# Working out the nodes' order in six pieces across a tile loop, with VectorE's order in that loop kept as written

## The chip, the cores and the metric

One NeuronCore of a Trainium2 chip runs the whole program. The metric is the device time in microseconds of one execution; lower is better. A profile of one further execution, with its own time, goes with it.

## What is computed

Four graph layers over 2048 nodes, 8 batches and 64 features, each with a residual and a layer normalization. The change concerns the first layer only, in which each node belongs to some of 64 hyperedges (`H` is 2048 x 64, zeros and ones):

```python
h = x @ W
s = leaky_relu(h @ a_node, 0.2)
alpha = softmax(where(H.T[None] > 0, s[:, None, :], NEG), axis=-1)
agg = einsum('ben,bnf->bef', alpha, h)
beta = sigmoid((h @ a_gn)[:, None, :] + (agg @ a_ge)[:, :, None])
all_he = elu(beta[..., None] * h[:, None] + (1 - beta[..., None]) * agg[:, :, None])
...
g = einsum('bne,benf->bnf', softmax(where(H[None] > 0, se[:, None, :], NEG), axis=-1), all_he)
```

The later layers multiply by the 2048 x 2048 adjacency matrix many times; they are most of the kernel's time.

## The kernel before

The 2048 nodes are 16 tiles of 128. The loop over h (lines 597 to 644, called the loop from here) takes one tile t in each turn:

- Four fp32 matmuls on TensorE (line 601) make `ph`, the products h of all eight batches with the two score columns beside them. `ph` has two buffers in PSUM, so tile t+2 can start only when tile t's `ph` has been read.
- VectorE clips the scores into `seen` (611), makes the leaky scores `lr` (618), writes (h+1) times an exponential into the staging tile `st` (624), and h times another exponential into `ex` (628). ScalarE (ACT) makes the two exponentials: `e_gn` out of `seen` (616), which `st` needs, and the column of `ex` out of `lr` (622), which `ex` needs.
- GpSimd (POOL) casts the tile's slot numbers into `st` (614).
- After every second tile, ACT's queue writes `st` to `hs_hbm` in memory (634). `st` has three buffers of two tiles each.
- Four matmuls (636) add the tile's part to `pagg`, the sums over the nodes of each hyperedge.
- At tiles 1, 3, 5, 7 and 9 POOL copies one element of `seen` (482) and then issues a load of part of the adjacency matrix (211): loads are paced by the loop in this way. At tiles 9 and 11 `parts` casts a piece of x on ACT (`v0h`, `v1h`, line 167) and subtracts on POOL (`v0l`, `v1l`, line 168).

A later stage handles nodes in the order of how many hyperedges they belong to, since nodes with few need few steps. `rank` (line 532) is each node's position in that order. `place()` (lines 553 to 590) turns it around: it finds for each node the tile `tl` of its position and the place `q` within it, makes the one-hot `ohq` (128 x 16 x 128) of the places, and the values `val` (the node's tile number and row, each under its `tl`). Sixteen small matmuls (582) sum `val` over the nodes into `po`, and `order` (589) holds, for each position, the node that belongs there. Everything but those matmuls is on VectorE. `place()` is called once, at tile 9 (line 631). `order` is read by the gathers of rows of `hs_hbm` (line 275), which POOL issues after the loop, and by the scatters of that later stage.

The program is written in a framework that decides itself in which sequence an engine gets its instructions, by their dependences and its own estimates. `tc.keep_in_program_order` marks an instruction to be kept in the sequence of the program among the others that are so marked. Before the change, in the loop, these are ACT's second exponential (622), POOL's paced copies and loads, the casts and subtractions of `parts(0, c)`, and the first instruction of `place()` (558); VectorE's four operations of a tile are not marked.

Of the kernel before, what the change touches and what calls it, by code (L numbers as in the profile page):

```python
# [30 lines left out]
F32 = mybir.dt.float32  # L31
F32R = mybir.dt.float32r
BF16 = mybir.dt.bfloat16
# [4 lines left out]
ALU = mybir.AluOpType  # L38
AX = mybir.AxisListType
# [17 lines left out]
def tile_gnn_fast(  # L57
# [24 lines left out]
    nc = tc.nc  # L82
# [3 lines left out]
    P = 128  # L86
    NT = N // P
# [116 lines left out]
    order = hy.tile([P, NT], U32, name="order")  # L204
# [4 lines left out]
    def load_adj(t, g):  # L209

        tc.keep_in_program_order(nc.gpsimd.dma_start(adj[t][g], adj_t[t * P:(t + 1) * P, cols(g, N // 2)]))
# [119 lines left out]
    xc, part = {}, {}  # L331
# [7 lines left out]
    def parts(p, c):  # L339
        part[c] = split(va, xc.pop((p, c)), f"v{c}", 1, [P, JT, P], nc.gpsimd, p == 0)  # L340
# [94 lines left out]
    with tc.tile_pool(name="pa_ps", bufs=1, space=PSUM) as pps:  # L435
# [17 lines left out]
        def fetch_xt(t):  # L453

            if t < NT:
                if t % (2 * XB) < XB:
                    xt[t] = xs.tile([P, NP, P], F32, tag="xt", name="xt", bufs=XB)
                else:
                    xt[t] = va.tile([P, NP, P], F32, tag=("v2h", "v2l", "v3h", "v3l")[t % XB], name="xt", bufs=1)
                nc.sync.dma_start(xt[t], x_t[t])  # L460
# [3 lines left out]
        so_scope = ExitStack()  # L464
        so = so_scope.enter_context(tc.tile_pool(name="so", bufs=1))
# [4 lines left out]
        iota = so.tile([P, P], BF16, name="iota")  # L470
        nc.gpsimd.iota(iota, [[1, P]], base=0, channel_multiplier=0, allow_small_or_imprecise_dtypes=True)
        row = so.tile([P, 1], F32, name="row")
# [8 lines left out]
        def behind(what):  # L481
            tc.keep_in_program_order(nc.gpsimd.tensor_copy(seen_x, what))
# [13 lines left out]
        for b in range(2):  # L496
# [21 lines left out]
            flat, lhsT=tri, rhs=oh.rearrange("p t b -> p (t b)"), start=True, stop=False  # L518
        )
        for t in range(NT - 1):  # L520
            nc.tensor.matmul(
                flat[:, (t + 1) * BINS:], lhsT=ones_b,
                rhs=oh[:, t:t + 1, :].to_broadcast([P, NT - 1 - t, BINS]), start=False, stop=False,
            )
        nc.tensor.matmul(
            flat, lhsT=ones_b, rhs=gtb[:, None, :].to_broadcast(bins), start=False, stop=True
# [4 lines left out]
        rank = so.tile([P, NT], F32, name="rank")  # L531
        nc.vector.tensor_reduce(rank, gt, AX.X, ALU.add)

        over = so.tile([P, BINS], F32, name="over")
# [9 lines left out]
        for t in range(NT // 2):  # L544
            for k in range(2):
                r = slice(k * E, (k + 1) * E)
# [6 lines left out]
        def place():  # L553

            tl = so.tile([P, NT], F32, name="tl")
            ge = so.tile([P, NT, NT], F32, name="ge")
            tc.keep_in_program_order(
                nc.vector.tensor_scalar(over[:, 0:NT], iota[:, 0:NT], float(P), -0.5, op0=ALU.mult, op1=ALU.add)
            )
            wide = [P, NT, NT]  # L560
            nc.vector.tensor_tensor(
                ge, rank[:, :, None].to_broadcast(wide), over[:, None, 0:NT].to_broadcast(wide), ALU.is_gt
            )
            nc.vector.tensor_reduce(tl, ge, AX.X, ALU.add)
            nc.vector.tensor_scalar(tl, tl, -1.0, None, op0=ALU.add)
            q = so.tile([P, NT], F32, name="q")
            nc.vector.scalar_tensor_tensor(q, tl, -float(P), rank, op0=ALU.mult, op1=ALU.add)
            nc.vector.tensor_tensor(
                ge, tl[:, :, None].to_broadcast(wide), iota[:, None, 0:NT].to_broadcast(wide), ALU.is_equal
            )  # L570
            val = so.tile([P, NT, 2, NT], BF16, name="val")
            nc.vector.tensor_tensor(
                val[:, :, 0, :], ge, iota[:, 0:NT, None].to_broadcast(wide), ALU.mult
            )
            nc.vector.tensor_scalar(val[:, :, 1, :], ge, row, None, op0=ALU.mult)
            po = pps.tile([P, 2, NT], F32, tag="sm", name="po", bufs=2)
            ohq = so.tile([P, NT, P], BF16, name="ohq")
            nc.vector.tensor_tensor(
                ohq, q[:, :, None].to_broadcast([P, NT, P]), iota[:, None, :].to_broadcast([P, NT, P]), ALU.is_equal
            )  # L580
            for t in range(NT):
                nc.tensor.matmul(
                    po.rearrange("p i t -> p (i t)"), lhsT=ohq[:, t, :],
                    rhs=val[:, t].rearrange("p i t -> p (i t)"), start=t == 0, stop=t == NT - 1,
                )
            olo = so.tile([P, NT], F32, name="olo")
            nc.vector.tensor_copy(olo, po[:, 1, :])

            nc.vector.scalar_tensor_tensor(order, olo, float(NT), po[:, 0, :], op0=ALU.mult, op1=ALU.add)
            so_scope.close()  # L590


        seen = pa.tile([P, NT, B, 2], F32, name="seen")

        pagg = pps.tile([P, C], F32, tag="agg", name="pagg", bufs=1)
        G = B // 2
        for t in range(NT):
            ph = pph.tile([P, 2, C], F32, tag="ph", name="ph", bufs=2)
            ph8 = ph.rearrange("p k (g c) -> p (k g) c", c=P)
            for p in range(NP):  # L600
                nc.tensor.matmul(
                    ph8[:, 2 * p:2 * p + 2, 0:F + 2], lhsT=xt[t][:, p, :], rhs=bd66, start=True, stop=True
                )
            fetch_xt(t + 2 * XB)
            hv = ph8.rearrange("p (k g) c -> p k g c", k=2)
            if t % 2 == 0:
                st2 = pa.tile([P, 2, HROW], F32, tag="st", name="st", bufs=3)
            st = st2[:, t % 2]
            ex = pa.tile([P, 2, G, F + 1], F32, tag="ex", name="ex", bufs=2)
            sv = seen[:, t].rearrange("p (k g) c -> p k g c", k=2)  # L610
            nc.vector.tensor_scalar(
                sv, hv[:, :, :, F:F + 2], CLIP, -CLIP, op0=ALU.min, op1=ALU.max
            )
            nc.gpsimd.tensor_copy(st[:, BF + 8:], slot[:, t, :])
            e_gn = st[:, BF:BF + 8]
            nc.scalar.activation(e_gn.rearrange("p (k g) -> p k g", k=2), sv[:, :, :, 1], AF.Exp)
            lr = pa.tile([P, B], F32, tag="lr", name="lr", bufs=2)
            nc.vector.scalar_tensor_tensor(
                lr, seen[:, t, :, 0], 0.2, seen[:, t, :, 0], op0=ALU.mult, op1=ALU.max
            )  # L620
            tc.keep_in_program_order(
                nc.scalar.activation(ex[:, :, :, F], lr.rearrange("p (k g) -> p k g", k=2), AF.Exp)
            )
            nc.vector.scalar_tensor_tensor(
                st[:, 0:BF].rearrange("p (g f) -> p g f", f=F), ph8[:, :, 0:F], 1.0,
                e_gn[:, :, None].to_broadcast([P, B, F]), op0=ALU.add, op1=ALU.mult,
            )
            nc.vector.tensor_tensor(
                ex[:, :, :, 0:F], hv[:, :, :, 0:F], ex[:, :, :, F:F + 1].to_broadcast([P, 2, G, F]), ALU.mult
            )  # L630
            if t == 9:
                place()
            if t % 2:
                nc.scalar.dma_start(hs_hbm.rearrange("(p t) c -> p t c", t=NT)[:, t - 1:t + 1, :], st2)
            for k in range(2):
                nc.tensor.matmul(
                    pagg[k * E:(k + 1) * E, 0:G * (F + 1)], lhsT=m_n[:, t, :], rhs=ex[:, k].rearrange("p g c -> p (g c)"),
                    start=t == 0, stop=t == NT - 1,
                )
            if t in paced:  # L640
                behind(seen[:, t, 0, 0:1])
                load_adj(paced[t], 0)
            if t in (9, 11):
                parts(0, (t - 9) // 2)
# [25 lines left out]

        gv = pagg[:, 0:G * (F + 1)].rearrange("p (g c) -> p g c", c=F + 1)
        den = ta.tile([P, G], F32, name="den")
        nc.vector.tensor_scalar(den, gv[:, :, F], 1.0e-30, None, op0=ALU.max)
        nc.vector.reciprocal(den, den)
        agg = ta.tile([P, G, F], F32, name="agg")
        nc.vector.tensor_tensor(agg, gv[:, :, 0:F], den[:, :, None].to_broadcast([P, G, F]), ALU.mult)
# [64 lines left out]
    with ExitStack() as pb_scope:  # L741
        pps = pb_scope.enter_context(tc.tile_pool(name="pb_ps", bufs=1, space=PSUM))
# [94 lines left out]
    pin = tc.keep_in_program_order  # L837
# [505 lines left out]
    def load_raw(k, place):  # L1343
        raw[k] = xnp.tile(wide_w, F32, tag=f"xn{place}", name="raw")
        pin(nc.sync.dma_start(raw[k], w_8[k]))
# [415 lines left out]
    place = ["g"] * NCH  # L1761
# [63 lines left out]
    for p in range(NP):  # L1825
# [3 lines left out]
        for step in range(STEPS):  # L1829
# [4 lines left out]
            for g in range(2):  # L1834
# [16 lines left out]
                for mine in ([[c] for c in own] if very_end else [own]):  # L1851
                    for t in range(NT if p or step else 0):
                        if checks and t in (2, 7, 12):
                            check()
                        for i in range(2):
                            for c in mine:
                                mm(
                                    u[c], lhsT=x_part[t // JT][i][:, t % JT, :], rhs=adj_c(t, c),
                                    start=False, stop=t == NT - 1 and i == 1,
# [765 lines left out]
```

## Time and profile before

| what | value |
|---|---|
| time, median of 3 runs | 1736.24 us (1735.61, 1736.24, 1749.89) |
| profiled execution: its own time | 1743.63 us |
| profiled execution: span | 1741.8 us |
| mean granted clock of TensorE | 0.987 |
| first `seen` of the loop | at 14.77 us |
| last `ex` of the loop ends | at 56.26 us |
| place(): first instruction to end of `order` | 34.40 to 42.04 us |
| first gather of rows (POOL) | issued at 59.39 us |
| DMA, 16.4 to 36.5 us | 382 GB/s, share 1.06 |

Times in the profile are counted from the start of the span. PE is TensorE's matmuls, PEld its weight loads, DVE is VectorE, ACT ScalarE, POOL GpSimd; SPq, ACTq and POOLq are the queues in which DMAs are issued. L624 is line 624 of the kernel. An entry such as `st<-ph,st 128x512` names the tile written, the tiles read, and the partitions and elements. The idle time in brackets lies before the instruction on its engine, with what ended it. A duration can overlap the start of the next instruction on the same engine a little. The granted clock is the share of TensorE's full clock that it was given.

### The profile page before, as it was taken

The numbers are of one execution on the slowest core, as the hardware profiler recorded it, in microseconds if no ns is written. First come the engines' busy times: TensorE is split into PE (matmuls) and PEld (weight loads), VectorE is DVE, ScalarE is ACT, GpSimd is POOL, SyncE is SP. The second block draws the span as 40 slices with busy tenths as digits, with TensorE's granted clock in tenths as the row PEclk, the third lists the DMA queues.
The fourth block names the chain that finished last, engine by engine and source line by source line (L and its number), as shares of the span: only waits on it lengthen the run. The fifth ranks groups of instructions, "written<-read, shape, count | busy, mean of one in ns | idle before, by whom it ended". The sixth has DMA issues, their size and how long they took to land. (4 is left out here: it accounts for less than half of the span.)

```text
span 1741.8 us, 27973 instructions
## 1 busy us (share of the span) xinstructions
PE 1659.0 (95%) x11196; PEld 1208.1 (69%) x11196; DVE 833.1 (48%) x1531; ACT 589.4 (34%) x1031; POOL 572.4 (33%) x515
## 2 busy tenths in 40 slices
PE   6889899999989999999999999999989999999996
PEld 4657666666664444468788878888767877878775
DVE  7678945677742221210127247777623433433332
ACT  1345533434322211112123267878512222212221
POOL 4578845566534444422023001322310200202001
PEclk9899999999999999999999999999999999999998
DMA  9744334444340000017344367575671121211211
GB/s 336 252 158 124 107 123 145 139 147 132 107 151 6 30 7 24 25 54 291 120 143 124 109 152 159 131 171 123 157 265 43 51 59 43 61 48 42 57 43 39
DMA packets 171180, 195.83 MB, mean 112 GB/s; under 512 B 71536, under 2 KB 116336, under 8 KB 169760
## 3 DMA queue, kind: packets, MB, share of 16 engines
q1 hardware_dynamic: 160096, 154.54, 30.5%
q0 software_dynamic: 8544, 30.68, 5.3%
q10 hardware_dynamic: 2400, 8.72, 1.3%
q8 instruction: 90, 1.47, 0.4%
q14 instruction: 50, 0.41, 0.1%
HBM read 126.72 MB, written 67.17 MB: 111 GB/s over the span
## 5 line engine op out<-in xcount | busy, mean ns | idle before, releaser
L172 PE MATMUL ua<-pt,xn 128*128 128x512 f32 x512 | 230.2, 592 | 1.4 <-DVE pt L1151 1.4
L172 PEld LDWEIGHTS ua<-pt,xn 128*128 128x128 f32 x512 | 96.9, 190 | 111.1 <-issue 104.0
L1516 DVE COPY w_half<-pw 128x512 f32<-128x512 f32 x160 | 109.7, 705 | 86.2 <-PE pw L172 85.4
L1512 ACT COPY w_half<-pw 128x1024 f32<-128x1024 f32 x128 | 129.9, 1015 | 56.9 <-PE pw L172 56.8
L172 PE MATMUL py<-w_half,xg 128*32 128x128 f32 x4096 | 142.2, 279 | 1.2 <-issue 1.2
L172 PE MATMUL u<-adj,v0h 128*128 128x512 f32 x384 | 134.5, 428 | 1.1 <-ACT h L1820 1.1
L172 PE MATMUL u<-adj_more,v2h 128*128 128x512 f32 x384 | 126.1, 406 | 0.0
L172 PE MATMUL u<-adj,v0l 128*128 128x512 f32 x384 | 125.0, 403 | 0.0
L172 PEld LDWEIGHTS py<-w_half,xg 128*32 128x32 f32 x4096 | 111.3, 138 | 18.8 <-issue 1.9
L172 PE MATMUL u<-adj_more,v2l 128*128 128x512 f32 x384 | 124.3, 401 | 0.0
L1157 POOL TENSOR_TENSOR acc<-acc,pt 128x512 f32<-128x512 f32 x60 | 76.5, 1274 | 104.3 <-DVE pt L1151 103.6
L172 PE MATMUL pw<-est,wst 64*128 64x256 f32 x1024 | 110.0, 317 | 0.7 <-ACT w_half L1512 0.4
L1151 DVE TENSOR_SCALAR pt<-pt 128x512 f32<-128x512 f32 x64 | 29.9, 466 | 152.4 <-ACT pt L1150 152.3
L172 PEld LDWEIGHTS pw<-est,wst 64*128 64x128 f32 x1024 | 82.2, 184 | 25.6 <-ACT w_half L1512 18.4
L1729 ACT CAST ar<-fcav 128x512 fp32r<-128x512 f32 x64 | 39.6, 618 | 168.9 <-DMA fcav<-in_adj_t 168.0
L1730 DVE SCALAR_TENSOR_TENSOR ar<-fcav,ar 128x512 f32<-128x512 f32 x64 | 45.8, 715 | 102.4 <-ACT ar L1729 102.4
L172 PE MATMUL u<-adj_more,v3l 128*128 128x512 f32 x288 | 93.1, 399 | 1.2 <-DVE v3l L168 1.2
L172 PE MATMUL u<-adj,v1h 128*128 128x512 f32 x288 | 93.7, 403 | 0.0
L1150 ACT ACTIVATE pt<-s 128x512 f32<-128x512 f32 x64 | 38.0, 598 | 164.5 <-PE s L172 164.5
L172 PE MATMUL u<-adj_more,v3h 128*128 128x512 f32 x288 | 92.7, 400 | 0.0
L172 PE MATMUL u<-adj,v1l 128*128 128x512 f32 x288 | 92.0, 397 | 0.0
L1701 POOL TENSOR_TENSOR x<-x,rows 128x512 f32<-128x512 f32 x16 | 22.5, 1430 | 211.4 <-PE pt L175 127.8
(408 smaller groups left out, 3275.7 us busy)
## 6 DMA issues: line engine op xcount, KB each, us to landing
fcav<-in_adj_t SPq DMA_DIRECT2D x64, 256.0 KB, 3.0
u_hbm<-ut SPq DMA_DIRECT2D x48, 256.0 KB, 3.7
xg<-u_hbm SPq DMA_DIRECT2D x24, 512.0 KB, 7.7
adj<-in_adj_t POOLq DMA_DIRECT2D x16, 512.0 KB, 7.8
adj_more<-in_adj_t POOLq DMA_DIRECT2D x16, 512.0 KB, 9.8
adj_hbm<-adj_more SPq DMA_DIRECT2D x16, 512.0 KB, 6.2
x_hbm<-r SPq DMA_DIRECT2D x28, 256.0 KB, 2.3
hs_hbm<-st ACTq DMA_DIRECT2D x8, 584.0 KB, 4.8
```

The costliest lines, as they stand in the source:

```text
L172: tc.keep_in_program_order(nc.tensor.matmul(*args, **kw))
L1150: nc.scalar.activation(pt, s, AF.Exp)
L1151: nc.vector.tensor_scalar(pt, pt, 1.0, None, op0=ALU.max)
L1157: nc.gpsimd.tensor_tensor(accs[c], accs[c], pt, ALU.add)
L1512: pin(nc.scalar.copy(dst, pw.rearrange("p j o n -> p n (j o)")))
L1516: pin(copy(dst[:, :, 2 * j:2 * j + 2], bank.rearrange("p o n -> p n o")))
L1701: nc.gpsimd.tensor_tensor(xs, xs, b2.to_broadcast([P, JT, P]), ALU.add)
L1729: nc.scalar.copy(ar, seen_a)
L1730: nc.vector.scalar_tensor_tensor(ar.bitcast(F32), seen_a, 1.0, ar.bitcast(F32), op0=ALU.mult, op1=ALU.not_equal, accum_out=left[:, t, k:k ...
```

## The change

`place()` no longer emits its instructions at once. It is called before the loop, allocates its tiles, and returns six functions under the numbers of the tiles at whose end, behind `ex`, they are called: 8 (the tile of each position), 9 (the place in it, and the first half of `val`), 10 (the second half of `val`, and `ohq` for eight tiles), 11 (`ohq` for the other eight), 12 (the sixteen matmuls), 13 (`order`). `ohq` is made by two instructions instead of one. All VectorE instructions of these pieces, and the four of each tile in the loop, are marked to be kept in program order. Cut to its core:

```diff
-            tc.keep_in_program_order(
-                nc.vector.tensor_scalar(over[:, 0:NT], iota[:, 0:NT], float(P), -0.5, op0=ALU.mult, op1=ALU.add)
-            )
...
+            def tiles_of():
+                pin(nc.vector.tensor_scalar(
+                    over[:, 0:NT], iota[:, 0:NT], float(P), -0.5, op0=ALU.mult, op1=ALU.add
+                ))
+                pin(nc.vector.tensor_tensor(
+                    ge, rank[:, :, None].to_broadcast(wide), over[:, None, 0:NT].to_broadcast(wide), ALU.is_gt
+                ))
+                pin(nc.vector.tensor_reduce(tl, ge, AX.X, ALU.add))
+
+            def places_of():
+                pin(nc.vector.tensor_scalar(tl, tl, -1.0, None, op0=ALU.add))
+                pin(nc.vector.scalar_tensor_tensor(q, tl, -float(P), rank, op0=ALU.mult, op1=ALU.add))
+                pin(nc.vector.tensor_tensor(
+                    ge, tl[:, :, None].to_broadcast(wide), iota[:, None, 0:NT].to_broadcast(wide), ALU.is_equal
+                ))
+                pin(nc.vector.tensor_tensor(
+                    val[:, :, 0, :], ge, iota[:, 0:NT, None].to_broadcast(wide), ALU.mult
+                ))
+
+            def columns(part):
+                if part == 0:
+                    pin(nc.vector.tensor_scalar(val[:, :, 1, :], ge, row, None, op0=ALU.mult))
+                n = NT // 2
+                r = slice(part * n, (part + 1) * n)
+                pin(nc.vector.tensor_tensor(
+                    ohq[:, r, :], q[:, r, None].to_broadcast([P, n, P]), iota[:, None, :].to_broadcast([P, n, P]),
+                    ALU.is_equal,
+                ))
+
+            def sum_up():
+                for t in range(NT):
+                    nc.tensor.matmul(
+                        po.rearrange("p i t -> p (i t)"), lhsT=ohq[:, t, :],
+                        rhs=val[:, t].rearrange("p i t -> p (i t)"), start=t == 0, stop=t == NT - 1,
+                    )
+
+            def order_of():
+                pin(nc.vector.tensor_copy(olo, po[:, 1, :]))
+
+                pin(nc.vector.scalar_tensor_tensor(
+                    order, olo, float(NT), po[:, 0, :], op0=ALU.mult, op1=ALU.add
+                ))
+                so_scope.close()
+
+            return {
+                8: tiles_of, 9: places_of, 10: lambda: columns(0), 11: lambda: columns(1), 12: sum_up, 13: order_of
+            }
...
+        steps_of = place()
+        pin = tc.keep_in_program_order
         for t in range(NT):
...
-            nc.vector.tensor_scalar(
+            pin(nc.vector.tensor_scalar(
                 sv, hv[:, :, :, F:F + 2], CLIP, -CLIP, op0=ALU.min, op1=ALU.max
-            )
+            ))
...
-            if t == 9:
-                place()
+            if t in steps_of:
+                steps_of[t]()
```

The other three VectorE instructions of a tile (618, 624, 628) are wrapped in `pin` in the same way.

## The prediction

> **What bounds the kernel now.** I read the page first, then the order of time around the changed code, then the granted clock in short stretches, then the list of who waited for whom.
>
> The page, its head and TensorE's row of forty slices:
>
> ```profile
> span 1741.8 us, 27973 instructions
> ...
> PE 1659.0 (95%) x11196; PEld 1208.1 (69%) x11196; DVE 833.1 (48%) x1531; ACT 589.4 (34%) x1031; POOL 572.4 (33%) x515
> ...
> PE   6889899999989999999999999999989999999996
> ```
>
> TensorE bounds the kernel nearly everywhere, but not in the first slices of 43.5 us, and the loop over h runs from 14.8 to 56.3 us. What can be won lies in those 41 us. The order of time inside the loop (start, duration, engine, line; the bracket is idle time and its releaser):
>
> ```profile
> 34.40 0.17 DVE L558 TENSOR_SCALAR over<-iota 128x16 f32<-128x16 bf16 x1
> ...
> 36.32 2.32 DVE L578 TENSOR_TENSOR ohq<-q,iota 128x2048 bf16<-128x2048 f32 x1
> 36.53 2.20 POOL L614 CAST st<-slot 128x64 f32<-128x64 bf16 x1
> 38.57 1.68 DVE L572 TENSOR_TENSOR val<-ge,iota 128x256 bf16<-128x256 f32 x1
> ...
> 38.71 1.25 POOL L168 TENSOR_TENSOR v0l<-xc,v0h 128x512 fp32r<-128x512 f32 x1
> ...
> 41.88 0.16 DVE L589 SCALAR_TENSOR_TENSOR order<-olo,po 128x16 uint32<-128x16 f32 x1
> ...
> 45.25 0.17 DVE L611 TENSOR_SCALAR seen<-ph 128x16 f32<-128x16 f32 x1 [1.56 <-PE ph L601]
> ...
> 47.65 0.17 DVE L611 TENSOR_SCALAR seen<-ph 128x16 f32<-128x16 f32 x1 [2.02 <-PE ph L601]
> ...
> 47.96 0.69 DVE L624 SCALAR_TENSOR_TENSOR st<-ph,st 128x512 f32<-128x512 f32 x1
> ```
>
> Two things are to be seen. The order of the nodes holds VectorE from 34.40 to 42.04, and tile 10's st and ex stand behind it. And VectorE's sequence is not that of the program: it takes seen of tile 12 at 45.25, then waits for tile 13's ph, and only at 47.96 does tile 12's st. The same happens at the start: seen of tile 0 is at 14.77, seen of tile 1 at 16.38, st of tile 0 only at 16.67. From tile 4 to tile 8 the sequence is the program's, and seen goes from 23.39 to 30.62: 1.81 us a tile.
>
> TensorE in stretches of about 3.4 us (busy us and count of PE, PEld, DVE, ACT, POOL; granted clock; share of DMA; GB/s):
>
> ```profile
> 36.50:39.90 3.40, 0.00 (x0) 0.10 (x1) 3.40 (x2) 0.00 (x0) 3.40 (x3) 1.00 1.01 375
> 39.90:43.30 3.40, 1.87 (x21) 0.99 (x21) 3.21 (x10) 0.43 (x2) 0.47 (x3) 0.50 0.42 130
> 43.30:46.75 3.45, 3.45 (x14) 2.44 (x15) 0.73 (x3) 1.04 (x3) 1.27 (x1) 0.50 0.53 188
> 46.75:50.16 3.41, 1.71 (x14) 1.13 (x13) 2.48 (x6) 0.42 (x2) 0.00 (x0) 1.00 0.20 65
> 50.16:53.60 3.44, 3.44 (x15) 2.44 (x15) 1.86 (x5) 0.42 (x2) 0.00 (x0) 0.51 0.45 179
> 53.60:57.00 3.40, 2.00 (x16) 1.02 (x14) 1.92 (x6) 1.31 (x4) 0.00 (x0) 1.00 0.14 56
> ```
>
> After a stretch without matmuls the clock is 0.50 for two stretches; after one with 1.71 of 3.41 us busy (50%) it is 0.51 for one; after 2.00 of 3.40 (59%) it stays at 1.00. At half clock the eight ph matmuls of two tiles take 2.13 us instead of 1.17, the four of pagg 1.14 instead of 0.66. The waits between 14 and 57 us add up what this costs:
>
> ```profile
> DVE seen L611 <- PE ph L601: 8.5, 10, 2.0
> ...
> PE pagg L636 <- DVE ex L628: 6.5, 6, 1.7
> ...
> PE po L582 <- DVE val L575: 4.2, 1, 4.2
> ```
>
> VectorE and TensorE stand waiting for each other in turn. From seen of tile 8 (30.62) to the end of ex of tile 15 (56.26) are 25.64 us, where eight tiles at 1.81 would take 14.5.
>
> [...] L572, [...] took 1.68 us while v0l ran for 1.25 on POOL, where the 256 elements of L568 took 0.42, and the cast at 36.53 took 2.20 beside ohq. [...]
>
> **The change, part by part.** No instruction goes except that ohq becomes two; no DMA is added or dropped.
>
> *Pieces.* Durations by the rows of before: tile 8 gets 0.17+0.42+0.42 = 1.01 us; tile 9 0.17+0.17+0.42+0.42 = 1.18 (0.42 for L572 without its stall, as for L568); tile 10 0.34+1.22 = 1.56; tile 11 1.22; tile 12 sixteen small matmuls, 0.59 on TensorE (half of that at full clock by ratio, about 0.3, beside VectorE's 1.63 for the tile: nothing taken; uncovered it would be 0.6); tile 13 0.17+0.16 = 0.33. Where VectorE has a piece it no longer waits for ph: a tile's four operations take 0.21+0.21+0.61+0.60 = 1.63 start to start, so 0.18 of the 1.81 is cover for a piece.
>
> *Locks.* The ACT order puts the v0h cast (0.62) behind ex of tile 9, so v0l runs beside tile 9's piece[...]: I take the full 1.25. v1l comes likewise at tile 11's half of ohq; either POOL waits (nothing) or VectorE (1.25); I take 0.6. Bounds: 0 to 2.5. The casts of slot, 0.24 each, run several tiles ahead and hide.
>
> *Periods, clock full.* Tile 8: 1.81+1.01-0.18 = 2.64; 9: 1.81+1.18-0.18+1.25 = 4.06; 10: 3.19; 11: 1.81+1.22-0.18+0.6 = 3.45; 12: 1.81; 13: 1.96; 14: 1.81; 15 to the end of ex: 1.63. Sum 20.6 us.
>
> *Clock.* TensorE's work for a tile is 0.59+1.10 = 1.69 warm: 64% of tile 8's period, 42, 53 and 49% of the next. By the 50 and 59% above, the clock falls somewhere in 9 to 11. There it costs nothing as long as VectorE takes as long as TensorE's 3.14 (1.06+2.08) at half clock; afterwards one tile runs at 3.14 instead of 1.81: 1.3 us. Bounds: 0 and, in all of tiles 12 to 14, 4.0.
>
> *Fixed order.* In the tail it is in the periods already. At the start, ex of tile 0 can end at about 16.5 instead of 17.95, so ph of tile 2 starts at 17.2 instead of 18.59: 1.4 us. But DMA is busy at a share of 1.06 with 382 GB/s from 16.4 to 36.5, and st buffers come free by the hs writes (the cast of tile 6 waited 3.4 us for one, landing just ahead of its tile at 26.92). I take half, 0.7; bounds 0 and 1.4. Kept in order, a waiting VectorE instruction holds all behind it: if st waits for a write of hs, the next seen waits, and behind it ACT's exponentials and POOL's paced loads.
>
> *Sum.* 25.64 - 20.6 - 1.3 + 0.7 = 4.4 us less. What follows the loop starts from its end: pagg of tile 15 (56.32), the normalization on VectorE, and the last write of hs (issued at 55.74), behind which POOL holds both gathers of rows (59.39) and the remaining adjacency loads (64.36). order is then ready many us before the gather. I see nothing that holds to an absolute time, so I carry 4.4 through: span 1741.8 to 1737.4, the profiled execution 1743.63 to 1739.2; the median of the runs, 1736.24, lies 7.4 below that execution, and becomes 1731.8.
>
> **Rivals.**
> *More than that.* No lock stall (1.85 less), full clock (1.3 less), all of the start (0.7 more): 8.3 us, 1728. For it: in the steady part POOL's casts cost VectorE nothing visible. Against: 42% busy at tile 9 is below what dropped the clock before.
> *Hidden anyway.* The loop is shorter but the start's gain is lost to DMA and the clock stays halved through tiles 12 to 14: 25.64-20.6-4.0 = 1.0 us, 1735.2. For it: the DMA share of 1.06. Against: from 53.6 the share is only 0.14, so the last write of hs is not crowded.
> *Slower.* The clock is at half from tile 8 on and in the first window behind the loop: TensorE's 3.14 becomes the least period. 3.14+4.06+3.19+4.1+3.74+3.14+3.14+1.63 = 26.1 us (full locks, po's 0.6 uncovered), 0.5 over today, less the start's 0.7, plus 1.7 for one halved window of 3.4 in the next stage: 1.5 over, 1737.8. It decides once every window from tile 8 to behind the loop is halved; one full window that TensorE needs brings it back to even. For it: four tiles of low TensorE load in a row. Against: today's clock recovers after one full window.
> *Not as said.* If VectorE's sequence did not follow the program, only the pieces would be spread: about the second rival.
>
> **How the numbers follow.** Forecast (2.5 to 6 us less) 0.60; more 0.12; hidden 0.15; slower 0.13. Range: from 1727 (the second bound of gain and a little run spread) to 1740 (the slower case, and part of the spread of the runs shown, 1735.61 to 1749.89). The likeliest case alone gives 1730 to 1734. One per cent, 17.4 us, is about what a measurement can tell from no change, and no case above reaches it; I leave 0.02 on each side for a rearrangement of the later instructions that aren't kept in order, which I can't price, and 0.96 between.
>
> **What would show it.** Right: no seen before the tile's own st and ex are done; the end of ex of tile 15 near 51.9; a first drop of the clock around tiles 9 to 11; L572 or L568 long beside v0l. Wrong: the loop's end moves but hrow's gather does not; st waits for a write of hs and stops VectorE; or the stage from 66 us on takes longer by what the loop won.

## The result and the profile after

The kernel after takes 1735.3 us (median of 22 runs, 1727.48 to 1741.74); the kernel before took 1740.74 on the same chip (22 runs, 1735.61 to 1749.89). The ratio is 0.9971 with a 95% interval of 0.996 to 0.9981, which is 5.05 us less (1740.74 times 0.0029), within 1%. The forecast was 4.4 us less. Its 1731.8 us for the median stands 3.5 us too low all the same, since it counts from a median of three runs, 1736.24, and 22 runs of the kernel before give 1740.74. The profiled execution after took 1736.35 us with a span of 1734.6 and a mean granted clock of 0.987.

The page of the kernel after, its head and TensorE's row of slices:

```profile
span 1734.6 us, 27974 instructions
...
PE 1656.1 (95%) x11196; PEld 1206.1 (70%) x11196; DVE 833.3 (48%) x1532; ACT 589.4 (34%) x1031; POOL 570.6 (33%) x515
...
PE   6889899999989999999999999999989999999996
```

Nothing of size can be seen here: one instruction more, the same digits in all forty slices. The change has to be looked for in the loop. The order of time there (start, duration, engine, line; L580 to L604 are the pieces, L641 is lr, L647 st, L651 ex, L275 the gather):

```profile
34.78 0.43 DVE L580 TENSOR_TENSOR val<-ge,iota 128x256 bf16<-128x256 f32 x1
...
36.83 1.87 DVE L586 TENSOR_SCALAR val<-ge,row 128x256 bf16<-128x256 f32 x1
...
37.24 1.29 POOL L168 TENSOR_TENSOR v0l<-xc,v0h 128x512 fp32r<-128x512 f32 x1
38.61 1.21 DVE L589 TENSOR_TENSOR ohq<-q,iota 128x1024 bf16<-128x1024 f32 x1
...
42.02 1.72 POOL L168 TENSOR_TENSOR v1l<-xc,v1h 128x512 fp32r<-128x512 f32 x1 [1.92 <-ACT v1h L167]
...
42.73 1.03 DVE L641 SCALAR_TENSOR_TENSOR lr<-seen 128x8 f32<-128x8 f32 x1
...
46.73 0.17 DVE L604 SCALAR_TENSOR_TENSOR order<-olo,po 128x16 uint32<-128x16 f32 x1
...
49.73 0.68 DVE L651 TENSOR_TENSOR ex<-ph,ex 128x512 f32<-128x512 f32 x1
...
53.54 1.22 POOL L275 DMA_INDIRECT hrow<-hs_hbm,order  x1 [9.80 <-DVE he L702]
```

`order` is finished 4.9 us later than before (46.90 against 42.04) and nobody minds: its first user, the gather, comes at 53.54. What counts is the last ex, which ends at 50.41 instead of 56.26, and the gather follows it by the same 3.13 us as before. Half of ohq takes 1.21; the forecast's 1.22 was its author's estimate (slot, L551, a VectorE instruction of 128x1024 too, took 1.22 in the profile of before). The two long entries on VectorE, 1.87 for L586 and 1.03 for L641, are its stalls beside POOL's v0l and v1l: L586 took 0.34 in vl_vector, where no subtraction runs beside it, and lr takes 0.17 at the next tiles.

The waits of the kernel after between 14 and 57 us (in total, times, longest), in the kernel before the three lines had 5.6, 6.5 and 8.5 us in total:

```profile
POOL st L637 <- DMA hs_hbm<-st: 12.7, 5, 4.6
...
PE pagg L659 <- DVE ex L651: 8.3, 9, 1.4
...
DVE seen L634 <- PE ph L624: 0.7, 4, 0.2
```

VectorE has nearly stopped waiting for TensorE (0.7 us after 8.5); TensorE waits for VectorE a little more (8.3 after 6.5). VectorE is the bound of the loop now: it is busy for 32.5 of its 36.5 us, TensorE for 26.7. POOL's wait for the writes of hs has doubled; at one tile it reaches VectorE (order of time, tile 6):

```profile
25.80 0.21 ACT L639 ACTIVATE st<-seen 128x8 f32<-128x8 f32 x1 [2.37 <-DMA hs_hbm<-st]
25.84 0.42 POOL L637 CAST st<-slot 128x64 f32<-128x64 bf16 x2 [4.62 <-DMA hs_hbm<-st]
...
26.10 0.69 DVE L647 SCALAR_TENSOR_TENSOR st<-ph,st 128x512 f32<-128x512 f32 x1 [1.10 <-ACT st L639]
```

ACT waits for a free buffer of st, and VectorE's st waits 1.10 us for ACT.

The granted clock (columns as in the prediction). In each of the fourteen profiles every change of the clock lies on a grid with a step of 3.41 us, and where that grid lies differs from one execution to the next (a window starts at 33.17 us in one profile of the kernel after, at 35.17 in the other). A step of it is called a window from here. The windows of the kernel after in the loop, and one of a second profile of it:

```profile
33.17:36.58 3.41, 1.85 (x13) 1.17 (x12) 3.18 (x10) 1.04 (x3) 1.83 (x7) 1.00 0.89 327
36.58:40.00 3.42, 1.87 (x17) 1.29 (x18) 3.38 (x5) 0.06 (x1) 2.23 (x5) 1.00 0.96 295
40.00:43.41 3.41, 2.13 (x28) 1.58 (x26) 3.31 (x6) 1.20 (x4) 1.49 (x2) 1.00 0.73 287
43.41:46.82 3.41, 1.97 (x16) 1.30 (x16) 3.27 (x10) 0.64 (x3) 0.32 (x1) 1.00 0.31 79
...
35.17:38.58 3.41, 1.76 (x12) 1.17 (x12) 3.31 (x9) 1.04 (x3) 2.52 (x5) 1.00 0.95 299
```

TensorE is busy for 54 to 62% of these windows of the first profile and keeps its full clock; no halved window is left inside the loop. In the second profile two windows have 1.76 us, 51%, and the clock stays up as well. Behind the loop the clock falls at 60.5 us in the first profile and stays halved for 10.2 us, more than in the profile of before at that place (3.4 us, from 67.2).

All profiles can be laid side by side by their milestones. Behind the loop, the kernels with no added instruction have the same sequence on every engine (the kernel before and the kernel after differ in nothing there), so only timing can differ. Where a run is given "against" a time, that is the kernel before on the same chip. In microseconds; in brackets how much of the stretch had a halved clock; "loop" is the first seen to the end of the last ex; "to 510" goes to the first matmul that makes ua, a third of the way through; "w_half" is the stage from VectorE's first to its last w_half copy:

| kernel | last ex ends at | loop | to 510 | w_half |
|---|---|---|---|---|
| before | 56.3 | 41.5 (10.2) | 461.8 (20.5) | 238.6 (0) |
| before_again | 56.2 | 41.7 (10.2) | 457.9 (17.1) | 238.9 (0) |
| before_third | 55.4 | 40.9 (10.2) | 458.7 (23.9) | 238.1 (0) |
| after | 50.4 | 36.5 (0) | 460.9 (23.9) | 240.0 (3.4) |
| after_again | 51.2 | 36.7 (0) | 457.3 (13.7) | 238.3 (0) |
| order_only | 51.7 | 37.4 (6.8) | 459.9 (27.3) | 238.1 (0) |
| order_only_again | 52.2 | 37.5 (6.8) | 457.5 (20.5) | 243.4 (6.8) |
| pieces_only | 51.9 | 37.5 (3.4) | 459.4 (20.5) | 237.9 (0) |
| vl_vector | 51.0 | 36.9 (3.4) | 460.9 (23.9) | 238.0 (0) |
| early | 49.1 | 34.4 (0) | 457.2 (17.1) | 237.9 (0) |
| early_vl | 49.3 | 34.8 (0) | 459.8 (23.9) | 237.6 (0) |
| paced_later | 49.2 | 34.3 (0) | 459.9 (20.5) | 238.2 (0) |
| before_busy | 53.3 | 39.0 (3.4) | 457.4 (17.1) | 246.0 (3.4) |
| ps_busy | 50.2 | 36.0 (0) | 464.1 (27.3) | 245.5 (0) |

One profile is one execution, and the column "to 510" shows what one execution can be off by: 457 to 462 us for the kernels with identical instructions there. Each kernel's own time is therefore taken from its many runs, and the loop from the profile, where it repeats to 0.8 us or better (before three times, the kernel after and order_only twice each).

### The profile page after: what moved, and what is told of

Its sections match the earlier page's. It is cut to its first block, busy times and chain, and to the rows that moved or that the text cites. A ratio compares the mean times of both kernels' runs of the same rounds, so it can differ in the third digit from the quotient of the medians.

```text
span 1734.6 us, 27974 instructions
## 1 busy us (share of the span) xinstructions
PE 1656.1 (95%) x11196; PEld 1206.1 (70%) x11196; DVE 833.3 (48%) x1532; ACT 589.4 (34%) x1031; POOL 570.6 (33%) x515
```

## Experiments: the two halves of the change

**The fixed order alone.** All six pieces stay at tile 9, VectorE's order is kept:

```diff
-            if t in steps_of:
-                steps_of[t]()
+            if t == 9:
+                for step in steps_of.values():
+                    step()
```

> VectorE's order kept as in the changed kernel, but all six pieces stand together at tile 9. Theory (most of the gain is the kept order: tile 0's st no longer behind tile 1's ph, tile 12's not behind tile 13's): about 3 us less than the kernel before, with the clock still halved after the 6 us in which TensorE gets nothing; last ex of the loop about 3 us earlier than before. Rival (the gain is the spreading, which keeps TensorE's clock up): within 1 us of the kernel before, last ex at 55 to 56 us.

Measured: 1737.29 us (14 runs) against 1738.31, ratio 1.0 (0.9987 to 1.0013). The loop lasts 37.4 us, 4 less than before. The fall of the clock is still there, and shorter (windows of order_only):

```profile
34.61:38.02 3.41, 1.11 (x15) 0.81 (x13) 3.34 (x7) 0.00 (x0) 2.22 (x5) 1.00 0.94 316
38.02:41.44 3.42, 0.84 (x10) 0.59 (x12) 2.62 (x10) 0.73 (x4) 1.82 (x3) 0.50 0.73 257
41.44:44.85 3.41, 3.41 (x16) 2.12 (x12) 1.60 (x5) 1.10 (x4) 1.27 (x1) 0.50 0.44 180
```

With the pieces in one block, TensorE has 1.11 us of work in a window (33%) and the clock halves for 6.8 us. The order alone thus takes 4 us from the loop in this profile, and next to nothing from the time of the runs. Because these two don't fit, it was run again on another chip:

> The kept order with all pieces at tile 9, a second time. Its first profile had a loop 4.0 us shorter than before's, yet its runs showed no gain. Theory (the loop is really shorter, and the runs give it back in halved windows: mean clock 0.001 below before's): loop 37 to 38 us again, runs 0 to 2 us less than before, their mean clock 0.0005 to 0.0015 below before's. Rival (the first profile was a lucky execution): loop 39 to 41 us. Second rival (the first runs were unlucky): loop 37 to 38 us, runs 3 to 4 us less than before with the same mean clock.

Measured: 1737.29 (14 runs) against 1738.4, ratio 0.9992 (0.9978 to 1.0006); loop 37.5. Both halves of the contradiction repeat. The table shows where one execution loses the gain: this second profile has the loop's 4 us still in hand when it reaches ua (first ua matmul at 509.7 us; before: 514.2 to 518.0), and then takes 243.4 us in the w_half stage instead of some 238, with a gap of 2.39 us on TensorE at 1019.6 that ends on nothing the profile shows, and 6.8 us of halved clock. The first profile has no such loss there, and its execution took 1735.71. That this is what holds the median of the runs back can't be said from two profiles. The mean granted clock over the runs, 0.9854 and 0.9861 against 0.9862 and 0.9866 of before, accounts for about 0.4 to 1.0 us at the slopes found below; some 2 to 3 us stay open.

**The pieces alone.** VectorE's operations are left to the framework:

```diff
-        pin = tc.keep_in_program_order
+        pin = lambda i: i
```

> Six pieces at tiles 8 to 13 as in the changed kernel, but the four VectorE instructions of a tile are not kept in program order. Theory (kept order gives most): about 2 us less than before, the start of the loop as before (st of tile 0 behind seen of tile 1). Rival (spreading gives most): 4 to 5 us less, as the changed kernel.

Measured: 1734.54 (22 runs) against 1738.31, ratio 0.9982 (0.9973 to 0.9991), 3.1 us less. Loop 37.5, with one halved window of 3.4 us. From seen of tile 8 to the end it takes 20.58 us against 24.9 to 25.9 of before and 21.1 to 21.2 of after. Up to tile 8 it takes 16.90 against 15.8 to 16.0, but that is where its halved window lies (17.3 to 20.7 us). before_busy below, with the sequence of before and a halved window at the same place (17.2 to 20.6), takes 16.80. So the sequence at the start, which is the old one (lr of tile 0, then seen of tile 1 ahead of st of tile 0), isn't shown to cost this microsecond; the window is.

Either part by itself brings some 4 us to the loop and both together bring 4.7 (mean of before 41.4, of after 36.6), so the two remove largely the same thing, VectorE and TensorE waiting for each other in turn. In the runs the gain of the pieces is clear of noise (3.1 us), that of the order alone is not. What the order adds to the pieces isn't shown: at the tail nothing, at the start 0.3 to 0.5 us (15.28 to 15.64 in the four profiles of after and order_only), and the intervals of pieces_only and of the kernel after overlap.

**The kernel after, again, on a third chip** (no edit):

> The changed kernel once more, beside the others on one chip. Theory (what a run takes depends on how many windows of TensorE's clock are halved in it, about 1.2 us each by the earlier runs): 4 to 6 us less than before with a mean granted clock 0.001 to 0.002 higher, and the last ex of the loop at 50 to 51 us in the profile whatever the run's time. Rival (only the loop's own work counts, the clock is the same in both): the same mean clock, 6 us less.

Measured: 1734.67 (16 runs) against 1738.25, ratio 0.9973 (0.996 to 0.9986), 4.7 us less. The first seen is at 14.45, not at 13.87 as in the first profile; so of the 0.9 us by which that one had come earlier than in before, most was one execution's luck, and the loop itself (36.5 and 36.7) is what repeats. The halved time behind the loop doesn't repeat: 10.2 us in the first, 3.4 in the second.

**The kernel before, twice** (no edit), to learn how far one profile of it can be trusted:

> The kernel before once more, for a second profile. Theory (halved windows of the clock fall differently in each execution, and the one profiled first, 1743.6 us against a median of 1738, had three of them in the loop): seen of tile 0 to the end of the last ex takes 39 to 41.5 us, shorter than the 41.5 of the first if fewer than three windows are halved between 35 and 57 us, by about 1.2 us for each. Rival (VectorE's order alone sets it): 41.5 us again, within 0.5.

> The kernel before a third time, same question and same expectations as for the second profile.

Measured: 1740.3 and 1736.73 us, one execution each. The 10.2 us of halved clock inside the loop are there all three times; behind it there are 3.4, 10.2 and 6.8 us. The three halved windows in the loop repeat; what lies behind it varies with the execution.

## Experiments: stalls, clock and the wait at tile 6

**Other tiles for the pieces.** The same six pieces at tiles 2 to 7, where v0l and v1l don't run:

```diff
-                8: tiles_of, 9: places_of, 10: lambda: columns(0), 11: lambda: columns(1), 12: sum_up, 13: order_of
+                2: tiles_of, 3: places_of, 4: lambda: columns(0), 5: lambda: columns(1), 6: sum_up, 7: order_of
```

> As the changed kernel, with the six pieces at tiles 2 to 7 instead of 8 to 13. Theory (two VectorE instructions of the changed kernel's tiles 10 and 12 stood 2.4 us for POOL's two subtractions, and tile 6 waits 1.1 us for a write of hs, so pieces ahead of the subtractions and beside that wait cost less): 6.5 to 8 us less than before, last ex 1.5 to 3 us earlier than in the changed kernel. Rival (VectorE and TensorE are both full there, a piece costs its own length wherever it stands, and the other instructions of tiles 10 and 12 stand for POOL instead): 5 us less, last ex within 0.7 us of the changed kernel's 50.4.

Measured: 1731.29 (8 runs) against 1738.31, ratio 0.9968 (0.9956 to 0.998), 5.6 us less, between the two forecasts. The loop is 34.4, another 2.1 to 2.3 shorter than in the two profiles of the kernel after. That isn't because the stalls have gone. L586 takes 0.34 us, not 1.87, but lr of tiles 12 and 13 now stands beside the subtractions:

```profile
40.39 1.26 POOL L168 TENSOR_TENSOR v0l<-xc,v0h 128x512 fp32r<-128x512 f32 x1
...
40.59 1.09 DVE L641 SCALAR_TENSOR_TENSOR lr<-seen 128x8 f32<-128x8 f32 x1
```

The other one takes 0.97. Without a stall lr takes 0.17, so 0.92 + 0.80 = 1.7 us of stalls are left of 2.4, as the rival said. The rest of the gain is idle time that VectorE no longer has: it waited 1.10 us ahead of st at tile 6 and 0.55 at tile 8 in the kernel after and waits at neither here, since it comes to tile 6 4.8 us later, behind the pieces (seen of tile 6 at 29.45 against 24.63). Together, 0.7 + 1.10 + 0.55, that is about the 2.1 to 2.3 us.

**The subtractions on VectorE.** v0l and v1l are taken from POOL, so that no subtraction of POOL runs beside VectorE's instructions, and VectorE pays for them:

```diff
-                parts(0, (t - 9) // 2)
+                parts(0, (t - 9) // 2, nc.vector)
```

(`parts` gets the engine as an argument and hands it to the subtraction.)

> As the changed kernel, with the subtractions that make v0l and v1l on VectorE instead of POOL. Theory (VectorE stands 1.5 and 0.9 us for POOL's subtractions; its own two subtractions cost about 0.65 each): last ex about 1 us earlier than the changed kernel's, time 5.5 to 6.5 us less than before. Rival (the long durations beside POOL are not stalls): 1.3 us later, time 3.5 to 4 us less than before.

Measured: 1734.23 (22 runs) against 1738.31, ratio 0.9976 (0.9965 to 0.9988), not told apart from the kernel after. Its order of time at the two places:

```profile
36.60 0.72 DVE L168 TENSOR_TENSOR v0l<-xc,v0h 128x512 fp32r<-128x512 f32 x1
...
38.94 0.34 DVE L586 TENSOR_SCALAR val<-ge,row 128x256 bf16<-128x256 f32 x1
```

The subtraction costs VectorE 0.72 us itself (the expectation's 0.65 was an estimate; ex and st, of 128x512 too, take 0.68 and 0.69 in the kernel after), and L586 falls from 1.87 to 0.34. From tile 8 to the end of ex it takes 20.29 us against 21.17 and 21.10: 0.9 less, about what theory gives (2.4 of stalls less 0.72 + 0.68 of work is 1.0; 0.6 with the 1.95 of stalls in after_again). So the stalls beside POOL's two subtractions (2.4 and 1.95 us) cost VectorE more here than the subtractions themselves (1.40). It doesn't come through in the loop as a whole (36.9), because more was lost up to tile 8 (16.61 against 15.37 and 15.64): st of tile 6 stood 2.29 us for a write of hs, where it stood 1.10 and 1.36 in the kernel after.

**Both edits together.**

> Pieces at tiles 2 to 7, and the subtractions of v0l and v1l on VectorE. Theory (pieces that meet no subtraction leave the lock's cost on tiles 10 and 12, and moving the subtractions adds 1.3 us of VectorE for 2.4 us of standing): 0 to 1 us less than with the pieces early alone, 6 to 7 us less than before. Rival[...]: 1 us more than the early pieces alone.

Measured: 1730.45 (6 runs) against 1738.25, ratio 0.995 (0.9931 to 0.9968), 8.7 us less. The loop, 34.8, is no shorter than early's: no instruction of VectorE stalls, but it does the two subtractions (0.69 each) and waits for their casts on ACT (0.50 and 0.51). This is the fastest version tried: faster than before by its interval, and 4.2 us below the kernel after on the same chip (medians of 6 and 16 runs; the two intervals against before overlap by a little, 0.996 to 0.9968). That it beats early is not shown: the two ran on different chips, and their intervals overlap.

**Loads later.** The paced loads of the adjacency matrix, suspected of holding up the writes of hs, come at later tiles:

```diff
-        paced = {1: 5, 3: 6, 5: 7, 7: 8, 9: 9}
+        paced = {5: 5, 7: 6, 9: 7, 11: 8, 13: 9}
```

> The changed kernel with the five paced loads of the adjacency at tiles 5, 7, 9, 11, 13 instead of 1, 3, 5, 7, 9. Theory (tile 6's st waits 1.1 us for a write of hs because loads crowd the DMA): no idle of VectorE for st at tile 6, seen of tile 7 about 1 us earlier, loop about 1 us shorter, time 0 to 1.5 us less than the changed kernel. Rival (the x tiles and the hs writes fill the DMA by themselves, or the later loads crowd the later writes): seen of tile 7 as before, or the wait comes at tiles 8 to 12; same time.

Measured: 1738.48 (14 runs) against 1740.77, ratio 0.9986 (0.9975 to 0.9996). The wait of st at tile 6 (1.10 and 1.36 us in the kernel after) is gone, so it came from the loads, and up to tile 8 the loop takes 14.41 us instead of 15.37 and 15.64. As a whole it falls to 34.3, 2.3 us below the kernel after; the other half lies behind tile 8 (19.86 against 21.17 and 21.10), where the stalls beside v0l and v1l are smaller (0.19 on L586 and 0.86 on lr). But of the loop's 7.1 us only 2.4 are in the time. One place where the gain goes is just behind the loop. The last write of hs is issued at 48.65 us, and the gather of rows follows it by 6.09 us:

```profile
54.74 1.07 POOL L275 DMA_INDIRECT hrow<-hs_hbm,order  x1 [9.80 <-DVE tab L739]
```

In the kernel after the gather follows that write by 3.65 us, in both profiles, and is at 53.54 and 54.32. So the gather of paced_later is no earlier than that of the kernel after. From 46 to 50 us the DMA share is 0.94 to 0.95 (0.59 and 0.23 in the kernel after): that fits the rival, that the later loads crowd the later writes. Whether this is what the runs lose isn't shown; the profiled execution took 1733.27, and no stage of it in the table is longer than in before.

**TensorE kept busy in the kernel before.** Nine matmuls whose results nobody uses are issued while VectorE makes the order:

```diff
+            idle = pps.tile([P, 2 * P], F32, tag="idle", name="idle", bufs=1)
+            for i in range(9):
+                nc.tensor.matmul(
+                    idle.rearrange("p (i t) -> p i t", t=NT), lhsT=ident,
+                    rhs=over[:, None, 0:NT].to_broadcast([P, NT, NT]), start=True, stop=True,
+                )
```

> The kernel before, with nine useless fp32 matmuls of 256 columns[...] on TensorE while VectorE works out the order; ph of tile 11 then comes behind the sixteen matmuls of po. Theory (TensorE's idle stretch there drops its clock and the tail of the loop pays for it): no halved window between 38 and 47 us, last ex 2 to 4 us earlier than before's 56.3, time 2 to 3 us less. Rival (the tail is slow by VectorE's order alone): last ex at 56 us or, for the later ph, at 57, time as before or 1 us more.

Measured: 1743.39 (22 runs) against 1738.25, ratio 1.003 (1.002 to 1.0041): slower by 5 us. Yet in the loop it does what was wanted (its stretches):

```profile
34.00:37.40 3.40, 3.40 (x18) 2.70 (x19) 3.21 (x11) 0.99 (x3) 2.04 (x6) 1.00 0.79 233
37.40:40.80 3.40, 2.94 (x13) 2.01 (x13) 3.40 (x3) 0.00 (x0) 3.03 (x2) 1.00 0.99 367
40.80:44.20 3.40, 3.17 (x36) 2.52 (x35) 3.10 (x9) 0.43 (x2) 0.41 (x2) 1.00 0.46 140
```

Where the kernel before fell to half clock, this one stays at 1.00, and the loop is 39.0 instead of 41.4 on average. Its one halved window lies at the start, ahead of the edit. From seen of tile 8 to the end, which is what the edit touches, it takes 22.20 us, where before takes 25.5 on average and after 21.1. So keeping the clock up is worth about 3.3 us there, three quarters of what the change wins in that stretch, as far as this arrangement tells (ph of tile 11 comes behind po in it). It can't be added to what the kept order wins, since that too shortens the halved time. The loss lies far away: the w_half stage takes 246.0 us instead of some 238.

**TensorE kept busy behind the loop of the kernel after.** Sixteen matmuls are added where the clock fell at 60.5 us:

```diff
+        for _ in range(4):
+            mm(pagg, lhsT=ident_r, rhs=tab2, start=True, stop=True)
...
-            ps = pps.tile([P, 12, 2, B], F32, tag="ps", name="ps", bufs=1)
+            ps = pps.tile([P, 32, 2, B], F32, tag="ps", name="ps", bufs=1)
...
+                if t == 0:
+                    mm(ps[:, 12:].rearrange("p s i b -> p (s i b)"), lhsT=ident_r, rhs=tab2[:, 0:320], start=True, stop=True)
```

> The changed kernel, with 16 useless matmuls beside and just ahead of the twelve small ones (ps) that follow the loop. Theory (the clock's drop at 60.5 us, for three windows, gave back about 2.4 of the 5.9 us that the loop had won): at most one halved window between 57 and 75 us, the stage behind the loop 1 to 2.5 us shorter, time 1 to 2 us less than the changed kernel beside it. Rival (that stage is set by VectorE and ScalarE, the clock costs it nothing): the same time, or 1 us more for the added matmuls.

Measured: 1742.03 (22 runs) against 1738.25, ratio 1.002 (1.0009 to 1.0032): slower, and 7.4 us above the kernel after on the same chip. The clock stays up for longer, to 67.5 us, and one window is halved instead of three. But the kernel after had one halved window there too in its second profile, with nothing added. The added matmuls stand in the way: VectorE's first step behind the twelve (R of the first tile) is at 63.41, against 62.57 and 62.71 in the two profiles of after, and the first scatter of rows comes at 103.81, against 103.50 and 101.60. And the w_half stage takes 245.5 us.

## Why the prediction was right, point by point

**Where the time was.** Right. The loop's end and the gather moved by the same 5.85 us in the profiles. Over the three profiles of before and two of after, the loop is 4.7 us shorter; the runs gained 5.05 and 4.7. Of the signs that were to show the forecast wrong one did come, st waiting for a write of hs and stopping VectorE (1.10 and 1.36 us at tile 6), without undoing the gain. One reading of the lines was off without consequence: each fp32 matmul of the loop stands as two in a trace (before: 128 records of ph for 64 in the program, 64 of pagg for 32), so the eight ph matmuls of 2.13 us are those of one tile, not of two (and the four of pagg stand for two in the kernel's text); the 1.69 us for a tile are right, since they were read off the starts. And the runs tell apart far less than the "one per cent" of the forecast, as the intervals show.

**The pieces' durations.** Right: 1.21 and 1.22 for the halves of ohq, and the small ones as in before.

**The stalls beside POOL.** The forecast calls them locks. That VectorE would stand beside the subtractions was right, the place wrong, and the place isn't fixed. Forecast: 1.25 at tile 9's piece and 0.6 at tile 11's. Measured in the first profile: nothing at tile 9 (L580 took 0.43, for v0l came later), 1.87 − 0.34 = 1.53 at L586 and 1.03 − 0.17 = 0.86 on lr of tile 12, 2.4 together against 1.85. In after_again v0l came a little earlier, L586 took 0.34, and lr of tile 10 stood in its place:

```profile
36.71 1.28 POOL L168 TENSOR_TENSOR v0l<-xc,v0h 128x512 fp32r<-128x512 f32 x1
36.76 1.26 DVE L641 SCALAR_TENSOR_TENSOR lr<-seen 128x8 f32<-128x8 f32 x1
```

That makes 1.09 + 0.86 = 1.95 us. What the instructions read doesn't sort them: the forecast went by L572, which reads two tiles of SBUF, as lr does (`seen` twice), while L586 reads one, of 256 elements, and a number for each partition, and stood all the same, for 1.53 us. L586 also begins 0.41 us ahead of v0l in the trace and needs only 0.34 by itself; that it was v0l that held it is read from vl_vector and after_again, where no v0l runs beside it and it takes 0.34, and what held it in those 0.41 us stays open. POOL lost next to nothing on v0l: it took 1.29 beside L586 and 1.26 in before_third, where no VectorE instruction was long beside it, while L586 stood for 1.53. v1l took 1.72; it begins inside the second half of ohq, which took its usual 1.22, so there POOL lost some 0.46 us. In order_only v0l begins inside ohq too: it took 2.23, and VectorE lost nothing (2.38 for both halves of ohq). vl_vector tests it: with the subtractions away from POOL the stalls go (L586 0.34, lr 0.17).

**The periods.** The forecast was 20.6 us from seen of tile 8 to the end, with 1.85 of stalls; measured are 21.17 and 21.10, with 2.4 and 1.95. The sum comes out closer than its terms: VectorE stood idle 0.55 and 1.11 us ahead of st of tile 8, which the forecast left out although before has it too (0.51 to 1.11 us in its three profiles), and the rest of the work took 0.5 and 0.7 us less than forecast.

**The clock.** Wrong. The step said "By the 50 and 59% above, the clock falls somewhere in 9 to 11", at a cost of 1.3 us. It didn't fall in the loop in either profile, so the 1.3 us were charged in vain. In the loop nothing contradicts these two shares. Over all fourteen profiles, take the windows at full clock that lie in the loop or reach into it. Those with TensorE busy for less than 50% (nothing to 46% in six profiles, just under 50% in one) were all followed by a halved one, and none with more than 51.2% was. Between 50.2 and 51.2% both happened; the second fall of the kernel before, at 50.1 us in its first profile, came after 50.2 or 50.3% in all three. What was wrong is the load that was set against them. The forecast took single tiles (42, 53 and 49%). But tiles 9 and 11 took 2.8 us each and not 4.06 and 3.45, since the stalls fell on tiles 10 and 12, and a window takes in parts of two or three tiles: the least busy one of the kernel after has 54%, and 51% in after_again. So it was close, and luck has a part in it. In vl_vector, whose one long wait for a write of hs left TensorE 46% of a window from 27.0 us, one window of the loop was halved. Behind the loop they don't hold: there the clock fell after a window of 75% (after: 57.1 to 60.5 us). What else decides I can't say from these runs.

**The start.** Half right. From the first seen to seen of tile 8 it took 15.37 and 15.64 us against 15.80 to 16.04: 0.4 less on average, where 0.7 was forecast. The sequence is the program's from the first tile on; order_only, which has it too, took 15.28 and 15.52. What ate the rest is what the forecast named as a danger: st at tile 6 stood 1.10 us behind a write of hs. paced_later took that wait away and the same stretch to 14.41.

**The sum.** 1.3 charged in vain, against 0.1 to 0.55 more of stalls, 0.3 less at the start and the idle time at tile 8: errors of both signs, which leave 4.4 forecast beside 4.7 measured in the loop. That the two agree to 0.3 us is in part luck.

**Carried through.** Right in the runs of the two kernels, but less firmly than I wrote. Everything behind the loop is issued in the same sequence, and the 5.85 us of the first pair of profiles had shrunk to 3.4 by 84 us, because after had two more halved windows right behind the loop. By the end the spans of that pair differed by 7.2, for the profiled execution of before lies high among its runs. "I see nothing that holds to an absolute time" missed that each execution meets the clock's windows at other places. The grid of 3.41 us lies elsewhere from one profile to the next, and the runs put a number on it: over the 22 runs of the kernel after, the time falls by 1.26 us for each 0.001 of mean granted clock (correlation −0.86), and over two sets of 53 runs of before by 1.19 (−0.72) and 0.88 (−0.58). One halved window of 3.41 us is 0.001 of the mean (3.41 times 0.5 over 1735). So such a window goes with about 0.9 to 1.3 us, as an estimate from these slopes: small against the kernel, about a quarter of this change. The mean clock rose from 0.9864 to 0.9888 with the change (on the chip of after_again), some 2.4 windows, where the loop itself lost three.

**The rivals.** "More than that", 8.3 us, got one of its three conditions, the full clock. "Hidden anyway" failed: the clock didn't stay halved; the DMA that it relied on took the start's gain only in part. "Slower" needed every window from tile 8 on halved; none was. "Not as said" failed: the sequence is that of the program. The order alone, though, ended about where "hidden" was (0 to 1.4 us), and for a reason that no rival named and that isn't settled.

## What to carry to other kernels

When two engines wait for each other in turn over a shared pair of buffers, cut a long block on one of them into pieces between its other work; in the loop that brought some 4 us, and so did the fixed sequence alone, while both together brought 4.7. Judge such a change by many runs and not by the loop: the fixed sequence alone gave no clear gain in the runs, and one stretch with the same instructions took 457 to 462 us in different executions. Place the pieces where the engine would otherwise stand: at tiles 2 to 7 the same pieces cost 2.1 to 2.3 us less than at 8 to 13, mostly because VectorE no longer waited for a buffer. Don't count on a stall to go with the piece that is moved: with the pieces away from POOL's subtractions 1.7 of 2.4 us of stalls were left, on another instruction of VectorE. And ask of a transfer that is put off what it will meet: the later loads took the loop from 36.5 and 36.7 us to 34.3, and the gather behind it came no earlier (54.74 against 53.54 and 54.32).

## What the runs showed of the hardware that was not expected

The clock's windows lie on a grid of 3.41 us that differs from execution to execution; in this loop the clock fell after every window at full clock in which TensorE was busy for less than 50%, and after none with more than 51.2% (see "The clock" above).

With a few matmuls more at the start, a stage that runs a thousand microseconds later was slower in both runs that added them. before_busy (9 added) and ps_busy (16 added) took 246.0 and 245.5 us in the w_half stage, all kernels without added matmuls 237.6 to 240.0 but for one execution of order_only with 243.4. The waits there, between 1010 and 1240 us, of ps_busy:

```profile
PEld py L172 <- issue: 7.7, 7, 2.2
PE py L172 <- issue: 6.3, 8, 2.0
```

and of the kernel after:

```profile
PE py L172 <- issue: 1.7, 1, 1.7
```

"issue" means that TensorE waited for nothing the profile shows. Gaps of ps_busy at 1081.9, 1112.2, 1172.3 and 1202.6 us lie about 2 us behind transfers of 16 KB on the queue that the profile calls "instruction" (q8; at 1079.9, 1110.2, 1170.2, 1201.0), which come about every 4 to 8 us in this stage; most of these have no gap behind them. What ties these gaps to the added matmuls isn't shown.
